# Query parts stored once, the value ring set in phase one, and phase one's weights loaded into sixteen tiles

## Chip, cores and metric

The kernel runs on one core of a Trainium2 chip. The time is the device time of one launch in microseconds, lower is better; a "time" here is the median of several launches, and a profiled launch gives the trace.

## The reference, cut to what matters

The input `x` has 32 sequences of 128 rows and 512 columns, `ctx_2048` the same shape. One decoder layer with three post-norm parts is computed, each followed by a layer norm of the sum with its input:

```python
x = _layernorm(x + _L0_attn_ref(x, Wq, Wk, Wv, Wo))        # 16 heads of 32, rope, causal softmax over 128 rows
x = _layernorm(x + _L0_xattn_ref(x, ctx, ctx, gamma))      # no projections
x = _layernorm(x + _L0_ffn_ref(x, w1, b1, ln_g, ln_b, w2, b2))

def _L0_xattn_ref(q, k, v, gamma):                         # q, k, v: (B, 128, 512)
    qh = q.reshape(B, 8, 16, 512); kh = ...; vh = ...      # 8 heads; 16 of the 128 rows are the head's width
    qk = jnp.einsum('bhdq,bhdl->bhql', qh, kh) / 4         # 512 x 512 scores for each head
    ret = jnp.einsum('bhql,bhdl->bhdq', softmax(qk), vh).reshape(B, 128, 512)
    return gamma * ret
```

The feed-forward part is a "1.58 bit" one: rows are normalized and quantized to 8 bit steps, weights to -1, 0 and 1; 512 to 2048 columns, silu, gelu, a layer norm over 2048, quantization again, and back to 512.

## The kernel before

The kernel has two phases, each a plan of its own. A `Plan` holds operations (`pl.op`) with an engine, a cost, the buffers they read and write and a priority. `Plan.run` sorts them while the program is built: it takes, again and again, the operation that can start first by the plan's own costs, ties within `slack` going to the lower priority, and issues it. Priorities are the batch's number plus an offset for each kind of operation (`OFF1`, `OFF2`), written out by hand. So the order of instructions on each engine is fixed when the program is built, and a change of an offset moves the order everywhere. Nearly all DMAs are issued by SP, in order: an SP instruction that waits holds up all that stand behind it. In the built program a DMA also waits for the DMA that stands eight places before it.

*Phase one* does self-attention for the 32 batches. `split_weight` (L302) loads the weights of Q, K, V and the output projection as sixteen 128x512 pieces; each is split into a high part (`hi`, a rounded copy by ACT L317 or DVE L315) and a low part (`lo`, the remainder, DVE L318). The staging tiles `wst` are four. `load` (L332) brings x twice, transposed (`xt`) and plain (`xs`). `stage_q` and `rope` project: twelve matmuls of 128x512 for each of q, k and v (`project`, L346). `stage_s` turns q and k (L430), makes scores (L447), masks and takes maxima on DVE (L459), exponentials on ACT (L465), and turns the weights again (L477). `stage_o` applies them to v (L496), projects with `wo` (L346 again, twelve matmuls), adds x and normalizes (x1, L519). `quantize_weights` makes the feed-forward weights beside this.

Cross-attention needs x1 and the context to more than bf16 precision, so `split3` (L349 to L365) writes each as three bf16 parts `sp` whose sum is the value: a cast on ACT (L354), a subtraction on POOL (L357), a cast (L359) and a subtraction (L361). A product of two such sums keeps six of its nine terms; they are stacked along the contraction, six times 16 rows:

```python
Q_PARTS = (0, 1, 2, 0, 1, 0)
K_PARTS = (0, 0, 0, 1, 1, 2)
for s, k in enumerate(parts):
    dma(kind, lambda s=s, k=k: nc.sync.dma_start(dst[s].rearrange("t h c -> h t c"), sp.t[:, k, :]), 131, (sp,), (), prio)
```

So a query or key goes to DRAM (`q_d`, `k_d`) as six 128 KB stores, each part as often as it is needed (L364).

*Phase two* does cross-attention and the feed-forward part. A batch has two groups `(b, g)` of four heads. Tiles `kp` and `qp` (four of each) have 96 rows of these parts and two more; they come by one DMA each (`load`, L656). `b1_` makes scores only for the row maxima: 16 units of one matmul (L677, 96 rows) and one DVE reduction (L681). `shift` turns the maxima (L691), splits them in two bf16 parts (`mhi`, `mlo`, L694, L695) and sends them by two 4 KB DMAs into the last two rows of `qp` (L700); the last two rows of `kp` hold ones. `b2_` then makes the scores a second time with the maximum subtracted by these two rows (L756, 98 rows), the exponential on ACT into tiles `ex` (L759) and the product with the values (L766). The value tiles `cT` are a ring of three, `vring`; half of a tile holds ones, so that the same matmul gives the denominator. Those ones are set by three POOL memsets (L616) once the pools of phase two are open. `final` divides and normalizes, `up_`, `gelu_` and `down_` do the feed-forward part (L925, L940 to L997, L1009).

*The seam.* When the last projection is issued, `early` (L577) frees the memory of the q, k and v weights, opens there the tiles `kp` and `qp`, and loads all four of each. All other memory of phase two lies over that of phase one, so a tile there can be written only when phase one's tiles and the stores from them are done.

Of the kernel before, what the change touches and what calls it, by code (L numbers as in the profile page):

```python
# [42 lines left out]
Q_PARTS = (0, 1, 2, 0, 1, 0)  # L43
K_PARTS = (0, 0, 0, 1, 1, 2)
# [19 lines left out]

CFG = dict(y0e='Pool', x2be='Pool', q2T=1, q1=2, tb2=3, boost=1.0, bank_mT='mx', bank_q1T='m', bank_z='m', bank_q2T='mx', bank_py='m', early=5, ssv=1, NQ=4, cT=3, f=2, num=1, x1=2, rden=2, x2=2, nb=32, mx=3, sT=3, acc=1, m=1, ex=8, mTe='DVE', acce='ACT', q1e='ACT', q2e='ACT', lne='Pool', ye='Pool', sce='Pool', mxw=1, stw=1, pair=1, z=3, xb=3, slack=0.05, last_lne='DVE', last_ye='DVE', last_sce='DVE', last_y0e='DVE', last_bank_mT='sT', last_bank_q1T='m', last_bank_z='sT', last_bank_q2T='mx', last_bank_py='sT', zm='PPPP', last_zm='FFFP', q1m='p', q2m='ad', last_q1m='d', last_q2m='ad')
OFF2 = {'SP.const': -264.67, 'x.kq': 390.3, 'SP.v': 77.29, 'PE.mx': -381.13, 'DVE.mx': 126.92, 'PE.mT': -632.22, 'DVE.mT': 8.23, 'SP.m': -156.28, 'PE.sT': -531.43, 'ACT.ex': -687.83, 'PE.pv': 37.38, 'ACT.acc': -737.17, 'SP.f': 49.63, 'SP.fd': 1119.71, 'SP.fn': 725.19, 'SP.fx': 343.0, 'DVE.rd': -172.57, 'SP.fr': -316.31, 'SP.fb': 17.98, 'Pool.y': -355.28, 'DVE.y': -82.99, 'Pool.yn': -277.59, 'DVE.c1': -57.25, 'Pool.c1': -358.01, 'Pool.c1m': -627.03, 'Pool.q1a': -78.8, 'Pool.x2b': 72.59, 'SP.q1T': -375.73, 'PE.c1': 39.79, 'DVE.z': -137.9, 'ACT.gelu': -406.78, 'DVE.nmu': -80.22, 'ACT.sq': -333.32, 'Pool.zn': -48.07, 'Pool.zt': 303.63, 'Pool.zb': -221.61, 'ACT.sq2': 252.58, 'DVE.am2': 91.79, 'Pool.c2': -682.87, 'Pool.c2m': -291.19, 'ACT.q2a': -262.61, 'DVE.q2a': -514.12, 'SP.q2T': 382.04, 'PE.c2': 86.97, 'DVE.c3': 17.23, 'Pool.c3': -278.83, 'Pool.c3n': 302.38, 'SP.out': 77.71, 'SP.kq': -42.69, 'DVE.yn': -735.62, 'DVE.c1m': 785.24, 'DVE.q1a': 467.22, 'DVE.zn': 550.15, 'DVE.zb': -508.13, 'DVE.c2m': -306.12, 'DVE.c3n': 99.96}
OFF1 = {'SP.x': 76.47, 'SP.w': -83.56, 'ACT.w': 1251.46, 'DVE.wl': 97.39, 'DVE.w': 1455.82, 'SP.wq': 258.11, 'ACT.wq': -501.07, 'DVE.wq': -718.11, 'PE.wq': 497.75, 'ACT.xh': -83.03, 'Pool.xl': -493.52, 'PE.qkv': 642.06, 'DVE.rope': -749.29, 'Pool.rope': 726.68, 'ACT.v': -277.88, 'SP.cx': 161.38, 'ACT.cs': 561.27, 'Pool.cs': 151.36, 'Pool.cs3': 444.12, 'SP.cs': -169.59, 'SP.ct': -341.75, 'ACT.ct': 5.76, 'SP.cv': 657.35, 'PE.qkT': -233.53, 'DVE.qkT': -713.26, 'PE.sc': 223.31, 'DVE.mask': -673.03, 'ACT.exp': 343.93, 'DVE.rd': 481.16, 'DVE.pr': 893.48, 'PE.prT': -342.18, 'DVE.prT': 602.51, 'ACT.prT': 121.56, 'Pool.pr': 38.32, 'PE.pv': 403.29, 'ACT.oh': 297.53, 'DVE.ol': -241.16, 'PE.wo': 645.28, 'DVE.y': -873.41, 'Pool.y': 255.11, 'Pool.x1': -113.85, 'SP.x1': 730.76, 'ACT.xs': 299.8, 'Pool.xs': -1039.81, 'Pool.xs3': 582.54, 'SP.xs': 975.4}
C1 = dict(pace=15.0, xs=4, pr=5, prT=7, ra=3, qkT=4, sp=3, spr=2, xhe='ACT', lne='Pool', s1e='Pool', s2e='ACT', cxl=-0.5, wq=3.0, nb=32, wst=4, mm=3, tr=3, sc=4, scc=1.1, po=1, pc=4, spe='ACT', cte='ACT', s3e='Pool', qke='DVE', pre=['DVE', 'DVE', 'Pool', 'Pool'], prTe=['DVE', 'ACT', 'ACT', 'ACT'], wl=24.0, slack=0.02)
# [14 lines left out]
class Plan:  # L83
# [34 lines left out]
    def op(self, kind, cost, fn, ins=(), outs=(), prio=0.0, lat=None, rel=0.0, join=False):  # L118
# [5 lines left out]
        o.deps, o.new = [], []  # L124
# [96 lines left out]
def decoder_kernel(ctx: ExitStack, tc: tile.TileContext, x, xT, cx, cxT, wqkT, wvT, woT, gamma,  # L221
# [28 lines left out]
    q_d = [dram.tile([6, XD, XH, D], BF16, tag=f"qd{b}", name=f"qd{b}") for b in range(NB)]  # L250
    c_d = [dram.tile([P, XD, NC * XH], F32, tag=f"cd{b}", name=f"cd{b}") for b in range(NB)]
    k_d = [dram.tile([6, XD, XH, D], BF16, tag=f"kd{b}", name=f"kd{b}") for b in range(NB)]


    with ExitStack() as st1:
# [38 lines left out]
        for name in ("mm", "tr", "sc", "po"):  # L294
            pl.tag(name, C1[name], group="bank")
        pl.tag("part", 2, wts, (P, 16))

        def dma(kind, fn, kb, ins=(), outs=(), prio=0.0, rel=0.0):
            pl.op("SP." + kind, max(0.55, kb / 340), fn, ins, outs, prio, 2.2 + kb / 340, rel)


        def split_weight(name, wts, src, cols):  # L302
# [3 lines left out]
            for j in range(cols // 512):  # L306
                sl = slice(j * 512, (j + 1) * 512)
                w = pl.buf("w")
                halves.append(w)

                def part(c, sl=sl, w=w):
                    t = pl.buf("wst")
                    dma("w", lambda: nc.sync.dma_start(t.t, src[:, c, sl]), 262, (), (t,), -1.0)
                    if c % 2:
                        pl.op("DVE.w", 0.34, lambda: nc.vector.tensor_copy(hi[:, c, sl], t.t), (t,), (w,), -1.0)  # L315
                    else:
                        pl.op("ACT.w", 0.48, lambda: nc.scalar.copy(hi[:, c, sl], t.t), (t,), (w,), -1.0)  # L317
                    pl.op("DVE.wl", 0.6, lambda: nc.vector.tensor_tensor(  # L318
                        lo[:, c, sl], t.t, hi[:, c, sl].bitcast(F32), ALU.subtract), (t,), (w,), -1.0)
                for c in range(NC):  # L320
                    part(c)
            return hi, lo, halves

        def en(e):
            return nc.vector if e == "DVE" else nc.gpsimd
# [6 lines left out]
        def load(b):  # L332
            at = b
            XS[b] = xt, xs = pl.buf("xt"), pl.buf("xs")
            dma("x", lambda: nc.sync.dma_start(xt.t, xT[b]), 262, (), (xt,), at, (b - 1.5) * C1["pace"])
            dma("x", lambda: nc.sync.dma_start(xs.t, x[b]), 262, (), (xs,), at, (b - 0.5) * C1["pace"])

        def project(kind, pq, parts, w, sl, wb, prio):
# [3 lines left out]
            for i in range(0, 12, m):  # L342
# [5 lines left out]
                pl.op("PE." + kind, 0.236 * m, mm, used + [wb], (pq,), prio)  # L348

        def split3(kind, v, dst, parts, prio):  # L350
# [12 lines left out]
            for s, k in enumerate(parts):  # L363
                dma(kind, lambda s=s, k=k: nc.sync.dma_start(dst[s].rearrange("t h c -> h t c"), sp.t[:, k, :]), 131,  # L364
                    (sp,), (), prio)  # L365

        def context(b):
# [3 lines left out]
            split3("cs", t, k_d[b], K_PARTS, at)  # L371
# [114 lines left out]
        def stage_o(b):  # L486
# [35 lines left out]
            split3("xs", x1, q_d[b], Q_PARTS, at)  # L522
# [46 lines left out]
        for b in range(NB1):  # L569
# [3 lines left out]
            stage_o(b)  # L573
        pl.slack = C1['slack']
        NQ = CFG['NQ']
        kring, qring = [], []

        def early():

            st2.close()  # L580
            qk = pool(ctx, "qk", side="right")
            for i in range(NQ):
# [5 lines left out]
                for t, d in ((k, k_d), (q, q_d))[:2 if i < min(CFG['early'], NQ) else 0]:  # L588
                    nc.sync.dma_start(t[0:NPR], d[i // 2][:, :, 4 * (i % 2):4 * (i % 2) + 4, :].rearrange(
                        "s t h c -> (s t) h c"))  # L590
# [494 lines left out]
```

## Time and profile before

| | |
|---|---|
| median of 3 launches | 1676.19 us (1674.02 to 1684.5) |
| profiled launch | 1675.28 us, its span 1673.5 us |
| busy: PE, DVE, ACT, POOL | 93%, 83%, 86%, 75% of the span |
| granted TensorE clock, mean | 0.973 |
| DMA | 258.71 MB, mean 155 GB/s; `kd<-sp` and `qd<-sp` 192 stores of 128 KB each |
| last projection of phase one, first score of phase two | 562.6 us, 585.55 us |

In the profile, times are microseconds from the span's start. PE is the matmul side of TensorE and PEld its weight loads; DVE is VectorE, ACT ScalarE, POOL GpSimd, and SPq stands for the DMA issues of SP. A line of the timeline is: start, duration, engine, line of the kernel and operation, output and input names, shapes, count, and in brackets how long the engine was idle before and what ended that. Matmul ends are modelled, so a busy PE may still run below its pace. The chain of waits is followed back from the last instruction. A DMA piece in it is the time from issue, or from the release, to landing.

### The profile page before, as it was taken

The page shows a single profiled execution, that of the slowest core. Times are in us where ns is not written, and L with a number is a line of the kernel's source. Part 1 is how long each engine was busy: PE and PEld are TensorE (multiplying, and loading weights), DVE is VectorE, ACT ScalarE, POOL GpSimd, SP SyncE. Part 2 cuts the span into 40 slices and gives each one's busy share as a digit, 9 for nine tenths or more (in the row PEclk, how much of TensorE's full clock was granted, in tenths as well). Part 3 has the DMA queues.
Part 4 walks back from the last instruction along what each step waited for, and adds up shares of the span by engine and source line. Part 5 has one row for each costly group of instructions (what it writes and reads, how often), then busy time and mean ns, then how long its engine had stood idle before and what let it go on. Part 6 is the DMA issues. An engine that isn't in the chain of part 4 may idle for free.

```text
span 1673.5 us, 30270 instructions
## 1 busy us (share of the span) xinstructions
PE 1551.4 (93%) x9540; PEld 785.0 (47%) x9540; DVE 1383.9 (83%) x3315; ACT 1432.7 (86%) x2950; POOL 1251.5 (75%) x1679
## 2 busy tenths in 40 slices
PE   6999999999999799999999999999999999999844
PEld 4878777777778333333333333333333333333211
DVE  6877776777777678899999989899899999998674
ACT  4889989899976367999989989899999999998963
POOL 3777778777787404679879888878978888986772
PEclk8999999999999799999999999999999999999977
DMA  6476677766664654355455345545544544544221
GB/s 226 163 236 232 226 231 244 255 233 214 209 208 153 185 177 122 93 129 145 113 133 147 105 129 139 131 115 139 142 110 128 153 110 134 149 122 123 69 62 50
DMA packets 235680, 258.71 MB, mean 155 GB/s; under 512 B 110072, under 2 KB 159224, under 8 KB 235136
## 3 DMA queue, kind: packets, MB, share of 16 engines
q1 hardware_dynamic: 235520, 256.78, 52.8%
q8 instruction: 75, 1.23, 0.3%
q14 instruction: 85, 0.70, 0.1%
HBM read 142.41 MB, written 92.81 MB: 141 GB/s over the span
## 4 chain that ended last, share of the span: by engine, by line
PE 41%; DVE 18%; POOL 16%; DMA 9%; ACT 8%; issue 7%; SPq 1%; POOLq 0%; ACTq 0%; DVEq 0%
PE banka L346 12%; DVE mt L681 8%; PE acc L766 7%; PE sT L756 6%; POOL z L972 6%; PE mx L677 5%; PE m L925 2%; DVE am L998 2%; PE banka L477 2%; DMA qd<-sp 2%; POOL z L794 2%; PE banka L447 2%; ACT pr L465 1%; ACT ex L759 1%; PE banka L496 1%
## 5 line engine op out<-in xcount | busy, mean ns | idle before, releaser
L681 DVE TENSOR_REDUCE mt<-mx 128x1 f32<-128x512 f32 x1024 | 643.4, 679 | 54.9 <-PE mx L677 52.9
L759 ACT ACTIVATE ex<-sT 128x512 f32<-128x512 f32 x1024 | 533.9, 615 | 77.9 <-PE sT L756 74.4
L677 PE MATMUL mx<-kp,qp 96*128 96x512 bf16 x1024 | 336.9, 386 | 21.5 <-DVE mt L681 17.7
L756 PE MATMUL sT<-qp,kp 98*128 98x512 bf16 x1024 | 320.7, 385 | 15.9 <-DMA qp<-mlo 13.3
L766 PE MATMUL acc<-ex,cT 128*32 128x512 f32 x2048 | 289.4, 637 | 0.0
L465 ACT ACTIVATE pr<-pr,nm 128x128 f32<-128x128 f32 x512 | 198.9, 394 | 4.1 <-DVE nm L459 4.1
L756 PEld LDWEIGHTS <-kp 98*128 98x128 bf16 x1024 | 90.3, 98 | 223.7 <-issue 125.1
L677 PEld LDWEIGHTS <-qp 96*128 96x128 bf16 x1024 | 96.3, 98 | 195.5 <-issue 95.1
L972 POOL TENSOR_TENSOR z<-z,bb_b 128x512 f32<-128x512 f32 x119 | 154.4, 1301 | 0.3
L972 POOL TENSOR_TENSOR z<-z,g_b 128x512 f32<-128x512 f32 x119 | 153.5, 1297 | 0.5
L459 DVE CUSTOM_DVE_ANT_0 pr<-banka,cmask 128x128 f32<-128x128 f32 x512 | 111.0, 286 | 35.9 <-PE banka L447 35.2
L1009 PE MATMUL m<-w2q,q2T 128*128 128x512 fp8e4 x464 | 116.7, 385 | 16.4 <-DMA q2T<-q 16.4
L766 PEld LDWEIGHTS acc<-ex,cT 128*32 128x32 f32 x2048 | 70.6, 184 | 114.1 <-issue 108.8
L925 PE MATMUL m<-w1q,q1T 128*128 128x512 fp8e4 x464 | 119.1, 378 | 2.7 <-DVE z L928 1.3
L1009 PEld LDWEIGHTS <-q2T 128*128 128x128 f16 x512 | 51.0, 101 | 104.5 <-DMA q2T<-q 34.9
L465 ACT ACTIVATION_READ_ACCUMULATOR pr<-pr,nm 128x1 f32 x512 | 98.0, 191 | 0.0
L794 POOL TENSOR_SCALAR z<-z,nmu,rs 128x512 f32<-128x512 f32 x119 | 94.5, 801 | 1.8
L361 POOL TENSOR_TENSOR sp<-spr,sp 128x512 bf16<-128x512 f32 x64 | 76.7, 1200 | 20.3 <-ACT sp L359 18.2
L928 DVE SCALAR_TENSOR_TENSOR z<-m,dq,b_b 128x512 f32<-128x512 f32 x116 | 85.0, 733 | 1.8 <-PE m L925 1.5
L925 PEld LDWEIGHTS <-q1T 128*128 128x128 f16 x512 | 49.2, 97 | 76.1 <-issue 19.9
L846 POOL TENSOR_TENSOR num<-num,rden 128x512 f32<-128x512 f32 x29 | 37.1, 1278 | 62.3 <-DMA rden<-rd 62.2
L346 PE MATMUL banka<-wqkh,xh 128*128 128x512 f32 x256 | 73.9, 411 | 10.3 <-ACT xh L388 10.3
(152 smaller groups left out, 3247.9 us busy)
## 6 DMA issues: line engine op xcount, KB each, us to landing
kd<-sp SPq DMA_DIRECT2D x192, 128.0 KB
qd<-sp SPq DMA_DIRECT2D x192, 128.0 KB
kp<-kd SPq DMA_DIRECT2D x64, 384.0 KB
qp<-qd SPq DMA_DIRECT2D x64, 384.0 KB
F<-f SPq DMA_DIRECT2D x64, 256.0 KB
xt<-in_xT SPq DMA_DIRECT2D x32, 256.0 KB
xs<-in_x SPq DMA_DIRECT2D x32, 256.0 KB
ct<-in_cxT SPq DMA_DIRECT2D x32, 256.0 KB
```

The lines of the kernel that those rows point to most:

```text
L346: nc.tensor.matmul(pq.t, parts[a].t[:, c, :], w[t][:, c, sl], start=k == 0, stop=k == 11)
L459: nc.vector.tensor_tensor_reduce(pr.t[:, c, :], sc.t[:, c * P:(c + 1) * P], cmask, -1.0, 3e38, ALU.add, ALU.min, nm.t[:, c:c + 1])
L465: nc.scalar.activation(pr.t[:, c, :], pr.t[:, c, :], AF.Exp, scale=-1.0, bias=nm.t[:, c:c + 1], accum_out=den.t[:, c:c + 1])
L677: nc.tensor.matmul(sc.t[:, j, :], q.t[0:NPR, h, (qc + j) * P:(qc + j + 1) * P], k.t[0:NPR, h, :], start=True, stop=True)
L681: pl.op("DVE.mx", 0.064 + 0.534 * W, lambda: nc.vector.tensor_reduce(mt.t[:, i:i + W], sc.t, AX.X, ALU.max), (sc,), (mt,), p, join=True)
L756: nc.tensor.matmul(sc.t[:, i, :], k.t[:, h, lc * P:(lc + 1) * P], q.t[:, h, :], start=True, stop=True)
L759: pl.op("ACT.ex", 0.052 + 0.426 * SW, lambda: nc.scalar.activation(ex.t[:, j:j + SW, :], sc.t, AF.Exp, scale=1.0 / XD ** 0.5), (sc,), (ex, ...
L766: nc.tensor.matmul(acc.t[32 * h:32 * h + 32, :], v.t[:, :, XH * lc + 4 * g + h], exs[h // 2].t[:, h % 2, :], start=lc == 0, stop=lc == NC - 1)
L794: pl.op(e + "." + p, cost + 0.1, lambda: en(e).tensor_scalar(o.t[:, sl], v.t[:, sl], sh.t, sc.t, ALU.add, ALU.mult), ins, outs, prio)
L925: nc.tensor.matmul(flat(pz)[:, i * 512:(i + 1) * 512], q1T.t[:, c, :], w1q[:, c, (n + i) * 512:(n + i + 1) * 512], start=c == 0, stop=c == ...
L972: pl.op(e + kind, 0.148 + 0.0021 * w if e == "Pool" else 0.05 + 0.00105 * w, lambda: en(e).tensor_tensor(t(), t(), other[:, sl], op), src, ...
L1009: nc.tensor.matmul(flat(py)[:, 0:D], q2T.t[:, c, :], w2q[:, c, :], start=c == 0, stop=c == NI - 1)
```

## The change

1. *Queries.* `q_d` holds the three parts once: three stores a batch in place of six. The tile `qp` is filled by three DMAs (48, 32 and 16 rows) that repeat a part three times, twice and once. Keys are still stored six times, as three operations of three, two and one DMAs, in another order of the terms.
2. *Weights of phase one.* The sixteen pieces go into sixteen tiles, seven of `prT`, five of `pr` and four of `wst` (the first two are not in use yet), so that no load waits for a split. The first `xt` gets a priority ahead of them. The low parts are split over DVE (ten) and POOL (six).
3. *Value ring.* The `cT` tiles move to the memory that `early` frees, and their ones are set there, in phase one.
4. *Carry.* Loads of the first four `kp` and `qp` become operations of phase one's plan that follow the stores they need and the last projection. `b1_` of the first group (`CARRY = 1`), with its `shift`, is planned in phase one, its scores in phase one's PSUM banks.
5. All offsets, and the `slack` of phase one (0.02 to 0.05), have new values.

```diff
-Q_PARTS = (0, 1, 2, 0, 1, 0)
-K_PARTS = (0, 0, 0, 1, 1, 2)
+Q_TIMES = (3, 2, 1)
+K_ROWS = (slice(1, 6, 2), slice(0, 5, 4), slice(2, 3))
...
-    q_d = [dram.tile([6, XD, XH, D], BF16, tag=f"qd{b}", name=f"qd{b}") for b in range(NB)]
+    q_d = [dram.tile([3, XD, XH, D], BF16, tag=f"qd{b}", name=f"qd{b}") for b in range(NB)]
...
+    def load_k(t, b, g):
+        nc.sync.dma_start(t[0:NPR], k_d[b][:, :, 4 * g:4 * g + 4, :].rearrange("s t h c -> (s t) h c"))
+
+    def load_q(t, b, g):
+        r = 0
+        for k, n in enumerate(Q_TIMES):
+            nc.sync.dma_start(t[r * XD:(r + n) * XD],
+                              q_d[b][k, :, 4 * g:4 * g + 4, :].unsqueeze(0).to_broadcast([n, XD, 4, D]))
+            r += n
...
+        stage = ["prT"] * C1["prT"] + ["pr"] * C1["pr"] + ["wst"] * C1["wst"]
...
                 def part(c, sl=sl, w=w):
-                    t = pl.buf("wst")
-                    dma("w", lambda: nc.sync.dma_start(t.t, src[:, c, sl]), 262, (), (t,), -1.0)
+                    tag = stage.pop(0)
+                    t = pl.buf(tag)
...
+                    dma("w", lambda: nc.sync.dma_start(flat_(), src[:, c, sl]), 262, (), (t,), -1.0)
...
-                    pl.op("DVE.wl", 0.6, lambda: nc.vector.tensor_tensor(
-                        lo[:, c, sl], t.t, hi[:, c, sl].bitcast(F32), ALU.subtract), (t,), (w,), -1.0)
+                    e = "Pool" if c == 3 or c == 1 and name != "wqk" else "DVE"
+                    pl.op(e + ".wl", 0.6 if e == "DVE" else 1.23, lambda: en(e).tensor_tensor(
+                        lo[:, c, sl], flat_(), hi[:, c, sl].bitcast(F32), ALU.subtract), (t,), (w,), -1.0)
...
-            dma("x", lambda: nc.sync.dma_start(xt.t, xT[b]), 262, (), (xt,), at, (b - 1.5) * C1["pace"])
+            dma("x", lambda: nc.sync.dma_start(xt.t, xT[b]), 262, (), (xt,), at if b else -1000.0, (b - 1.5) * C1["pace"])
...
-            for s, k in enumerate(parts):
-                dma(kind, lambda s=s, k=k: nc.sync.dma_start(dst[s].rearrange("t h c -> h t c"), sp.t[:, k, :]), 131,
-                    (sp,), (), prio)
+            for k, rows in enumerate(parts):
+                def put(k=k, rows=rows):
+                    for d in range(*rows.indices(6)):
+                        nc.sync.dma_start(dst[d].rearrange("t h c -> h t c"), sp.t[:, k, :])
+                n = len(range(*rows.indices(6)))
+                pl.op("SP." + kind, 0.55 * n, put, (sp,), (), prio, 2.2 + 0.4 * n)
...
-            split3("xs", x1, q_d[b], Q_PARTS, at)
+            split3("xs", x1, q_d[b], [slice(k, k + 1) for k in range(3)], at)
...
+        for i in range(NQ):
+            b, g = divmod(i, 2)
+            K[b, g], Q[b, g] = pl.buf("kp"), pl.buf("qp")
+            for t, load_, kind in ((K[b, g], load_k, "cs"), (Q[b, g], load_q, "xs")):
+                pl.op("SP.kq", 1.2, lambda t=t, load_=load_, b=b, g=g: load_(t.t, b, g), (), (t,), NB1 + b + 0.5 * g, 3.4,
+                      after=pl.kinds["SP." + kind][3 * b:3 * b + 3] + pl.kinds["PE.qkv"][-1:])
+            if i < CARRY:
+                b1_(b, g, NB1 + b + 0.5 * g)
...
         def early():
             st2.close()
             qk = pool(ctx, "qk", side="right")
+            for i in range(CFG["cT"]):
+                t = qk.tile([P, 2 * XD, NC * XH], F32, tag=f"cT{i}", name=f"cT{i}")
+                nc.gpsimd.memset(t[:, XD:], 1.0)
+                vring.append(t)
             for i in range(NQ):
...
                 nc.sync.dma_start(k[NPR:NROW], ones_d)
-                for t, d in ((k, k_d), (q, q_d))[:2 if i < min(CFG['early'], NQ) else 0]:
-                    nc.sync.dma_start(t[0:NPR], d[i // 2][:, :, 4 * (i % 2):4 * (i % 2) + 4, :].rearrange(
-                        "s t h c -> (s t) h c"))
...
-    vring = [cb.tile([P, 2 * XD, NC * XH], F32, tag=f"cT{i}", name=f"cT{i}") for i in range(CFG["cT"])]
-    for t in vring:
-        nc.gpsimd.memset(t[:, XD:], 1.0)
...
         for g in range(2):
-            b1_(b, g)
+            if 2 * b + g >= CARRY:
+                b1_(b, g, b + 0.5 * g)
```

## The prediction

> **What bounds the kernel now.** I read the page first: no engine is idle for long, so a gain must come from a place where the busy engines stand still together.
>
> ```profile
> span 1673.5 us, 30270 instructions
> PE 1551.4 (93%) x9540; PEld 785.0 (47%) x9540; DVE 1383.9 (83%) x3315; ACT 1432.7 (86%) x2950; POOL 1251.5 (75%) x1679
> ```
>
> Then the busy time by stage (columns: PE, PEld, DVE, ACT, POOL busy us, granted TensorE clock, DMA share, GB/s).
>
> ```profile
> 0.00:50.00 50.00, 33.46 (x209) 25.75 (x209) 32.09 (x88) 22.72 (x57) 20.57 (x32) 0.90 0.59 190
> 50.00:100.00 50.00, 50.00 (x418) 40.72 (x415) 40.64 (x181) 45.75 (x162) 36.53 (x40) 1.00 0.60 199
> 100.00:200.00 100.00, 99.02 (x824) 79.82 (x823) 74.38 (x312) 93.88 (x296) 76.77 (x91) 1.00 0.72 241
> ...
> 550.00:580.00 30.00, 24.68 (x107) 10.67 (x105) 22.98 (x43) 10.32 (x30) 15.37 (x22) 0.76 0.76 228
> 580.00:640.00 60.00, 51.95 (x263) 16.73 (x264) 42.09 (x74) 35.34 (x69) 6.84 (x13) 0.92 0.54 164
> ```
>
> The reader is to see two holes: the first 50 us, with half the matmuls of the next 50, and the seam near 580. In between phase one (to 562) runs on PE and ACT at once, and phase two (from 586) on PE, DVE and ACT, all over 90%.
>
> At the head the timeline gives the first batch, and the windows its clock (columns: PE busy, clock, DMA share, GB/s).
>
> ```profile
> 9.62 0.62 ACT L388 CAST xh<-xt 128x512 fp32r<-128x512 f32 x1 [2.69 <-DMA xt<-in_xT]
> 30.34 1.91 PE L346 MATMUL banka<-wvl,xh 128*128 128x512 f32 x4
> 32.17 1.71 PE L447 MATMUL banka<-qkT,qkT 32*128 32x128 f32 x32
> ```
>
> ```profile
> 20.00:22.00 2.00, 2.00 (x6) 0.50 0.58 163
> 34.00:36.00 2.00, 2.00 (x9) 1.00 0.65 172
> ```
>
> By 32.17 PE has done only the 36 projection matmuls of batch 0, each about 0.47 us instead of the 0.234 of later rows (a group of 20 takes 4.66).
>
> At the seam, the timeline:
>
> ```profile
> 574.43 4.06 PE L677 MATMUL mx<-kp,qp 96*128 96x512 bf16 x7 [0.21 <-DVE mt L681]
> 582.45 1.45 POOL L616 MEMSET cT<- 128x512 f32 x3 [9.06 <-DMA qd<-sp]
> 582.37 0.33 SPq L663 DMA_DIRECT2D cT<-cd  x1
> 583.42 0.57 SPq L700 DMA_DIRECT2D qp<-mlo  x1
> 585.55 1.44 PE L756 MATMUL sT<-qp,kp 98*128 98x512 bf16 x3 [7.06 <-DMA qp<-mlo]
> 586.22 1.58 ACT L759 ACTIVATE ex<-sT 128x512 f32<-128x512 f32 x3 [14.06 <-PE sT L756]
> ```
>
> The last wo matmul ends at 562.6. The last query store is issued by 577.4 and lands at 582.4; the value load waits for it, the two shift rows wait behind that load on SP, and PE starts the scores of phase two at 585.55, 23 us after phase one's last matmul. Only 24 maximum units (L677, L681) fill the hole.
>
> **The sum is made against** the profiled execution, 1675.3 us (span 1673.5 and 1.8 around it); the median of the three runs, 1676.2, is 0.9 above it.
>
> **Head.** All sixteen weight pieces get a tile of their own, so their loads no longer wait for a subtraction to free one of four tiles; xt of batch 0 is issued ahead of them. In 5 to 10 us the trace moved 329 GB/s, 0.8 us for a 256 KB piece. The first piece landed at 4.5 us; the last of xt, eight wqk pieces, ct and four wv pieces is thirteen places later, near 15. Six of sixteen subtractions go to POOL: DVE loses 6 x 0.69 = 4.1 us, POOL gains 6 x 1.27 = 7.6, and has the room (20.6 busy of 50). Working down the built order with these rows, batch 0's projections end near 22 us, or 26 if the clock stays at half, against 32. But xt of batch 1 now stands behind wo, cx and xs, the 20th load: 4.5 + 19 x 0.8 = 20 us (27 at the first slice's 226 GB/s). The built order puts 72 projection matmuls ahead of the first scores, not 36: scores near 31 to 35 us with 36 x 0.234 = 8.4 us more done. The lead is 9.4 us at most (1 us earlier as well); after the scores ACT must follow, and it was busy 5.3 us of the 10 between 40 and 50, so it can win some 4.7 + 1. I take -6; bounds -9.4 and +2 (xt late).
>
> The trace shows the clock at 0.50 in 20 to 22 and again at 28 to 32, after PE pauses of 3 and 2.6 us. The Trainium skill (TensorE: Matmul & The Clock Gate, The HAM clock gate) says that the clock opens after about 3.4 us of sustained work and closes after an idle window of that length. By that rule an unbroken feed would run the second half of batch 0 at full rate, and the head would gain nearer 9 than 6.
>
> **Middle of phase one.** PE's work for a batch is 48 x 0.234 + 1.10 + 1.01 + 6 x 0.435 = 15.95 us; from 100 to 500 it did 24 batches, 16.67 each: 23 us lost over 32 batches. Query stores drop from six to three a batch: 96 x 128 KB = 12.6 MB of 258.7 are gone, and at 0.6 an issue 1.9 us of SP time a batch. The other edits of the queue (key stores issued as three operations, still six DMAs) cost nothing, since SP is no bound. Query stores make 5.1% of the chain between 90 and 562, 24 us; half of it is the most to win. PE itself never waits for a DMA there (its listed waits, 11.6 us, are on ACT, DVE and POOL), and ACT at 94% keeps its pace. The carried group adds 16 x 0.22 = 3.5 us of PE. All offsets are new and I can't cost that order. Taken: -4; bounds -12 and +6.
>
> **Seam.** Three things move. The three memsets (1.45 us of POOL) go to the end of the last projection, ahead of POOL's work on batch 28, and stop waiting for stores. The first of 64 maximum groups (16 matmuls, 16 reductions of 0.6, a transpose, two splits, two 4 KB DMAs) runs among the last softmaxes. Its K and Q loads and the other three groups' (16 DMAs where eight were) stand on SP behind the last projection. This adds a wait: the carried group's first matmul waits for them, behind it on PE the transposes, pv and wo of batch 31. The loads are issued some 4 us after the last projection and land in 4 to 7.7 (the chain shows 7.67 for qp<-qd there); 24 wo matmuls and a transpose, 6 us, cover them, so 2 to 5 us may show, where before PE idled about 4 us for the same softmax.
>
> What does not go: the first ex tile lies over phase one's tiles, and the built program still has it wait for the last query store. From the last wo: ya, one reduction, statistics 2.9 us; POOL scale and x 1.8; two casts, a subtraction and another 3.6; three stores of 0.4 to 0.6 and 2.5 to 4.8 to land: 12.5 us, against 23.6 before (562.6 to 586.2). So -11; but 24 units were done by then and now 16, and to the first down projection the built order has 179 units from there, not 164: 15 x 0.217 = 3.3 us of PE back. Net -8; bounds -12 (POOL never backlogged) and 0 (POOL still busy with batches 28 to 30 when x is due, as x1 stores held it until 568.86 before).
>
> **Phase two.** Sixty later Q loads become three DMAs: 120 more issues of 0.43 us, 52 us of SP over 1,000 us. Queued behind each are the shift rows mhi and mlo, for which PE waits. They are covered as long as the ring of four K/Q tiles is a group ahead; at 92% busy engines and one batch per 32.1 us (666 to 1532 for batches 1 to 28) I take 0, bounds -5 and +15. Also -1 for tail and rest, bounds 4 either way.
>
> The row for an issue of qp<-qd is 0.43 us. The skill (DMA: Bandwidth & Descriptors, Bandwidth) speaks against the split: batch transfers to 1 MiB, since a DMA carries about 2 us fixed. By that rule 120 extra DMAs are 240 us of latency if they ran one after another; issued back to back they overlap, and by it the sum would change little.
>
> Sum: -6 - 4 - 8 - 1 = -19: 1675.3 - 19 = **1656 us**.
>
> **Rivals.** *Only the seam counts* (1664 to 1676, middle 1668): PE and ACT are both at their pace in phase one (15.5 us of ACT a batch), so head start and lighter DMA dissolve, leaving -8. For: ACT at 94%; PE waits on no DMA. Against: ACT's 4.7 us of idle time in 40 to 50.
> *All of it works* (1630 to 1646): -9 head, -12 middle, -11 seam, -2: 1641. For: 23 us are lost in phase one without a full engine. Against: retuned offsets would have to find them.
> *Slower*: the shift rows are issued late in phase two. Place: SP, behind three-part Q loads; price: two issues, 0.87 us, of PE waiting for qp<-mlo in each of 60 groups, 52 us, less 19: 1708. It decides from 0.6 us a group (19 + 17 over 60). For: PE and its weight loads already wait 31 us in all for mhi and mlo. Against: SP sits waiting for DVE mlo at L700 for 148.7 us, so it is mostly there in time.
> *The loads aren't at once*: in the built program a DMA waits for the one eight places before it. Eight pieces are in flight, twice the four of before; the gain of the head holds, so this has no time of its own.
>
> **How the numbers follow.** Forecast 0.48 (1646 to 1664), only the seam 0.24, all of it 0.15, slower 0.13. The median can tell about 1% from no change, 1659.4 and 1693: faster takes 0.15 and most of the forecast, 0.45; same has the rest of it, 0.03, and the seam's 0.24; slower 0.13 is the last rival. Range 1638 to 1680: it cuts the best of the second case and nearly all of the slower one.
>
> **What would show it.** First scores at 31 to 35 us after 72 projections; last wo near 553; ex some 12 us after it, with POOL's memsets before; batch pace of phase two still 32.1. Wrong if first ex comes 20 us after the last wo, if phase one needs 16.7 a batch and the head's lead is gone by 100 us, or if PE's waits for mlo exceed 60 us.

## The result, and the profile after

The changed kernel takes 1786.11 us (median of 4 launches, 1781.3 to 1787.59) against 1675.11 in the same comparison for the kernel before: the ratio of the means is 1.0652, with a 95% interval of 1.0599 to 1.0705. The forecast was 1656, its range ended at 1680. The profiled launch took 1781.3 us.

The same two lines of the page:

```profile
span 1779.5 us, 30353 instructions
PE 1581.2 (89%) x9540; PEld 788.5 (44%) x9540; DVE 1388.2 (78%) x3309; ACT 1433.0 (81%) x2950; POOL 1258.0 (71%) x1685
```

The busy times of DVE, ACT and POOL are those of before within 7 us; the span is 106 us longer. So the engines do the same work and stand still for longer. The busy time by stage says where (columns as in the prediction: PE, PEld, DVE, ACT, POOL, granted clock, DMA share, GB/s):

```profile
0.00:50.00 50.00, 39.49 (x224) 30.06 (x224) 36.09 (x101) 27.51 (x76) 35.32 (x45) 1.00 0.68 227
50.00:100.00 50.00, 49.05 (x468) 39.34 (x467) 40.28 (x175) 46.95 (x167) 33.85 (x38) 1.00 0.58 187
...
550.00:580.00 30.00, 12.40 (x73) 7.70 (x73) 13.35 (x24) 5.75 (x10) 11.53 (x15) 0.71 0.38 127
580.00:640.00 60.00, 51.35 (x227) 14.81 (x227) 41.37 (x71) 29.99 (x58) 0.00 (x0) 0.86 0.45 126
640.00:1550.00 910.00, 822.37 (x4150) 289.74 (x4147) 762.63 (x1291) 763.03 (x1151) 681.59 (x969) 0.95 0.52 116
```

The long stretch of phase two, 640 to 1550, was this before:

```profile
640.00:1550.00 910.00, 881.90 (x4600) 314.14 (x4599) 842.02 (x1428) 845.56 (x1280) 748.92 (x1066) 0.99 0.49 127
```

The head is better (39.49 us of PE where 33.46 were). The seam, meant to shrink, is emptier (12.40 where 24.68 were). And in the long stretch of phase two DVE and ACT each lose some 80 us of work against before. Its last two columns are the strange ones: before, the DMA engines were 0.49 busy and moved 127 GB/s; now they are 0.52 busy and move 116. More time in the engines for fewer bytes.

The chain of waits by engine, before:

```profile
PE 41%; DVE 18%; POOL 16%; DMA 9%; ACT 8%; issue 7%; SPq 1%; POOLq 0%; ACTq 0%; DVEq 0%
```

And after, by engine and by line:

```profile
PE 43%; DMA 18%; POOL 11%; ACT 10%; DVE 10%; issue 4%; SPq 3%; POOLq 0%; ACTq 0%; DVEq 0%
PE banka L436 11%; PE acc L798 8%; PE sT L788 7%; PE mx L301 6%; DMA rden<-rd 5%; POOL z L1004 4%; DVE mt L305 3%; DMA cT<-cd 3%; ACT pr L558 3%; PE m L1041 3%; DMA qp<-qd 2%; PE m L957 2%; PE banka L570 2%; SPq L286 2%; ACT ex L791 2%
```

DMA was 9% of the chain, 0.09 x 1673.5 = 151 us, and is 18%, 320 us. Transfers that were on nobody's path are on it now: rden (the reciprocal coming back), cT (values), qp. Pieces of that chain in order of time (start, duration, what):

```profile
750.62 8.15 DMA qp<-qd
...
786.70 9.01 DMA qp<-qd
...
862.70 13.47 DMA q2T<-q
...
907.99 7.59 DMA cT<-cd
```

Before, this was the longest piece of a transfer in phase two's chain:

```profile
1201.82 4.89 DMA rden<-rd
```

To split the loss by stage I read four marks from the timelines of the profiled launches: the end of the last q, k or v projection (the 562.6 given with the time before is the end of the output projection), the start of the first and of the last q1T transpose that SP issues, and the span's end.

| | last projection | to first q1T | first to last q1T | tail | span |
|---|---|---|---|---|---|
| before | 549.1 | 95.1 | 978.1 | 51.1 | 1673.5 |
| after | 540.7 | 121.1 | 1066.6 | 51.0 | 1779.5 |
| difference | -8.4 | +26.0 | +88.5 | -0.1 | +106 |

The tail is nothing, the head and the middle came out as forecast, and the seam and all of phase two went wrong together. What they share is the new Q load (L286).

### The profile page after: what moved, and what is told of

Read it like the earlier page. It is cut to its first block, busy times and chain, and to the rows that moved or that the text cites. A ratio compares the mean times of both kernels' runs of the same rounds, so it can differ in the third digit from the quotient of the medians.

```text
span 1779.5 us, 30353 instructions
## 1 busy us (share of the span) xinstructions
PE 1581.2 (89%) x9540; PEld 788.5 (44%) x9540; DVE 1388.2 (78%) x3309; ACT 1433.0 (81%) x2950; POOL 1258.0 (71%) x1685
## 4 chain that ended last, share of the span: by engine, by line
PE 43%; DMA 18%; POOL 11%; ACT 10%; DVE 10%; issue 4%; SPq 3%; POOLq 0%; ACTq 0%; DVEq 0%
PE banka L436 11%; PE acc L798 8%; PE sT L788 7%; PE mx L301 6%; DMA rden<-rd 5%; POOL z L1004 4%; DVE mt L305 3%; DMA cT<-cd 3%; ACT pr L558 3%; PE m L1041 3%; DMA qp<-qd 2%; PE m L957 2%; PE banka L570 2%; SPq L286 2%; ACT ex L791 2%
## 5 line engine op out<-in xcount | busy, mean ns | idle before, releaser
L305 DVE TENSOR_REDUCE mt<-mx 128x1 f32<-128x512 f32 x1008 | 636.4, 679 | 107.2 <-PE mx L301 104.1
L788 PE MATMUL sT<-qp,kp 98*128 98x512 bf16 x1024 | 323.6, 387 | 20.2 <-DMA qp<-mlo 11.3
L798 PE MATMUL acc<-ex,cT 128*32 128x512 f32 x2048 | 297.7, 657 | 18.5 <-DMA cT<-cd 18.3
L1041 PE MATMUL m<-w2q,q2T 128*128 128x512 fp8e4 x464 | 127.6, 413 | 24.4 <-DVE top L900 18.4
L1030 DVE TENSOR_REDUCE am<-z 128x1 f32<-128x2048 f32 x32 | 72.9, 2277 | 31.0 <-POOL z L1004 30.8
L840 POOL TENSOR_SCALAR rsa<-mv 128x1 f32<-128x1 f32 x64 | 13.8, 215 | 112.8 <-DVE mv L834 100.3
```

The lines of the kernel that those rows point to most:

```text
L305: pl.op("DVE.mx", 0.064 + 0.534 * W, lambda: nc.vector.tensor_reduce(mt.t[:, i:i + W], flat(sc).rearrange("p (a b) -> p a b", a=W), AX.X, ...
L788: nc.tensor.matmul(sc.t[:, i, :], k.t[:, h, lc * P:(lc + 1) * P], q.t[:, h, :], start=True, stop=True)
L798: nc.tensor.matmul(acc.t[32 * h:32 * h + 32, :], v.t[:, :, XH * lc + 4 * g + h], exs[h // 2].t[:, h % 2, :], start=lc == 0, stop=lc == NC - 1)
L1041: nc.tensor.matmul(flat(py)[:, 0:D], q2T.t[:, c, :], w2q[:, c, :], start=c == 0, stop=c == NI - 1)
```

## Experiments

**The theory.** A Q load reads `q_d[b][k, ...].unsqueeze(0).to_broadcast([n, XD, 4, D])`: the n copies, 3 or 2, are the slowest dimension, and the 16 rows stand inside. If the load is divided among the DMA engines along that dimension, only 3 or 2 of 16 engines carry it. It lands late, and whatever else passes those engines lands late behind it ("spread"). The rivals were the number of loads ("count": three where one was, with their issue time and the wait for the DMA eight places before) and the new offsets, carried group and seam ("order").

### The copies moved inside

```diff
-  q_d[b][k, :, 4 * g:4 * g + 4, :].unsqueeze(0).to_broadcast([n, XD, 4, D])
+  q_d[b][k, :, 4 * g:4 * g + 4, :].unsqueeze(1).to_broadcast([XD, n, 4, D])
```

The rows of K are stored in the matching order. Three loads stay, with the same bytes.

> The changed kernel with its three Q loads a group kept, same bytes and same order of work on all five engines, but inside each load the copies of a row lie next to each other (16 rows outermost, the 3 or 2 copies inside) instead of the 3 or 2 copies outermost; the K rows are stored to match. Theory 'spread' (a load whose slowest dimension is 3 or 2 is carried by 3 or 2 of the 16 DMA engines, lands late and holds up the transfers behind it): the loss of phase two goes, 1650 to 1675 us, PE's chain waits for rden<-rd, cT<-cd and qp<-qd fall to the 4 to 5 us they had before the change. Rival 'count' (three DMAs where one was, their issue time and the wait for the eighth DMA before): nothing changes, 1780 to 1792. Rival 'order' (offsets, carried group, seam): nothing changes, 1780 to 1792.

Measured: 1661.53 us, ratio to before 0.9942 (0.9919 to 0.9965). One changed pattern takes away 125 us (1786.11 to 1661.53); "count" and "order" fall as main causes. Against the kernel before, the whole change is now worth 0.6%. The same two views for this kernel, the stretch of phase two and the chain by engine:

```profile
640.00:1550.00 910.00, 885.39 (x4631) 318.14 (x4630) 842.05 (x1431) 851.04 (x1284) 753.30 (x1073) 0.99 0.50 127
```

```profile
PE 45%; POOL 16%; DVE 15%; ACT 12%; DMA 7%; issue 4%; SPq 1%; POOLq 0%; ACTq 0%; DVEq 0%
```

DVE, ACT and the bytes moved are back at the rate of before, and DMA is 7% of the chain.

### Six loads of 16 rows

```diff
-  nc.sync.dma_start(t[r * XD:(r + n) * XD],
-                    q_d[b][k, :, 4 * g:4 * g + 4, :].unsqueeze(0).to_broadcast([n, XD, 4, D]))
+  for i in range(n):
+      nc.sync.dma_start(t[(r + i) * XD:(r + i + 1) * XD], q_d[b][k, :, 4 * g:4 * g + 4, :])
```

> The changed kernel with six Q loads a group of 16 rows and 64 KB each in place of three (stored once as before, same order of work). 'Spread': each load has 16 rows outermost and the loss goes although there are 192 DMAs more, 1655 to 1695 us. 'Count': worse than the changed kernel, since the three added DMAs a group cost as much again, 1850 to 1900. 'Order': 1780 to 1800.

Measured: 1669.87 us (ratio 0.9985, 0.9967 to 1.0004). Twice as many loads, and 116 us faster than the changed kernel, with K stored as there. "Count" does have a price: 192 loads more cost 8.3 us against the version before this one, 0.04 us each.

### Storing undone, and storing alone

The first puts six stored copies and one 96-row load back into the changed kernel; the second puts the once-stored Q with its three loads, copies outermost, into the kernel before and changes nothing else there but the order of K's parts, to match. The first edit, cut to what matters:

```diff
- q_d = [dram.tile([3, XD, XH, D], ...
+ q_d = [dram.tile([6, XD, XH, D], ...
...
- for k, n in enumerate(Q_TIMES):
-     nc.sync.dma_start(t[r * XD:(r + n) * XD],
-                       q_d[b][k, :, 4 * g:4 * g + 4, :].unsqueeze(0).to_broadcast([n, XD, 4, D]))
...
+ nc.sync.dma_start(t[0:NPR], q_d[b][:, :, 4 * g:4 * g + 4, :].rearrange("s t h c -> (s t) h c"))
...
- split3("xs", x1, q_d[b], [slice(k, k + 1) for k in range(3)], at)
+ split3("xs", x1, q_d[b], [slice(0, 3), slice(3, 5), slice(5, 6)], at)
```

> The changed kernel with the storing of Q undone: six copies are written, one 96-row load a group; order of the other engines' work unchanged. 'Spread' and 'count' both: 1655 to 1680 us, the gain that the prediction gave to head and seam less its share for the lighter stores. 'Order': 1775 to 1795.

> The kernel before with only the storing of Q changed: stored once, three loads a group with the 3 or 2 copies outermost, everything else and the order of the other engines' work as before. 'Spread' and 'count': about as slow as the changed kernel, 1760 to 1800 us. 'Order': 1665 to 1680.

Measured: 1691.3 us and 1803.46 us. The second settles that this part alone makes a kernel slow: without any of the other edits it costs 131 us, and its phase two (first to last q1T) is 1104.6 us long. Which wait shows it depends on the order: here it is the shift rows, for which PE's second scores wait 79.6 us (who waited, for what, us in total, times, longest):

```profile
PE sT L768 <- DMA qp<-mlo: 79.6, 22, 15.1
```

The first missed its expectation by 11 us. Its phase two is sound (974.2), but its last projection ends at 562.9, 23 us later than with three stores (539.8 with the copies inside). In the changed order, three more stores a batch cost much more than the 4 us that the prediction gave them.

### Loads by themselves

A kernel that only loads. Each of 13 forms was issued alone, four times; the table has eleven of them.

> Only loads, nothing of the layer is computed: 13 forms of a load from device memory, each issued alone after the one before has landed, four times over; then four of them with a 256 KB load of 128 rows issued right behind. All 48-row forms carry the same 192 KB (48 rows of 4 KB). A small VectorE copy marks when a load is there, a GpSimd copy when the 256 KB behind it is. Theory 'spread': the head of the kernel before moved 329 GB/s, 20 GB/s for each of 16 engines, so the n-outermost form takes about 192 KB / n / 20 GB/s beyond a fixed part: against the plain 48 rows, n = 2 lands 4.2 us later, n = 3 2.6, n = 4 1.8, n = 6 1.0, n = 8 0.6, n = 16 none; copies inside (16 rows outermost) none; and the 256 KB behind n = 3 or n = 2 lands late by about the same. Rivals 'count' and 'order': all forms of 192 KB land within 0.4 us of each other and the load behind them does too.

The table gives the median time from the start of the issue to the start of the copy that waits for the load.

| form | KB | us | | form | KB | us |
|---|---|---|---|---|---|---|
| 48 plain rows | 192 | 2.88 | | 6 copies outermost | 192 | 4.25 |
| 3 copies inside | 192 | 3.31 | | 8, 12 copies outermost | 192 | 3.38, 3.41 |
| 2 copies outermost | 192 | 5.99 | | 16 copies outermost | 192 | 3.28 |
| 3 copies outermost | 192 | 5.85 | | 16 plain rows | 64 | 2.06 |
| 4 copies outermost | 192 | 3.97 | | 96 plain rows | 384 | 3.43 |

The 96 rows are twice the bytes in little more than half the time. How many engines work is in the DMA column of the windows, the mean busy share of 16 engines (last two columns: share, GB/s). The first window lies inside a load with 2 copies outermost, the second inside one with 3, the third inside one of 96 plain rows:

```profile
17.00:20.00 3.00, 0.00 (x0) 0.00 (x0) 1.00 0.12 44
23.50:26.50 3.00, 0.00 (x0) 0.00 (x0) 1.00 0.18 60
48.50:49.50 1.00, 0.00 (x0) 0.00 (x0) 1.00 0.68 229
```

Two engines of 16 are a share of 0.125 and three are 0.188; the windows show 0.12 and 0.18. The rate for one engine is the same in all three, 44 / (16 x 0.12) = 23, 60 / (16 x 0.18) = 21 and 229 / (16 x 0.68) = 21 GB/s, so nothing is wrong with the reading itself. The trace's semaphore events agree. Between issue and landing a DMA's semaphore is counted up 3 times with 2 copies outermost, 4 times with 3, 5 with 4, 7 with 6, 9 with 8, 13 with 12, and 16 times for every form with 16 or more rows or copies outermost: one signal for each engine at work, and one more where fewer than 16 are. (The Trainium skill, DMA: Bandwidth & Descriptors, "Why a DMA increments its semaphore by 16 and not by 1", says what the one more is: the issuer writes the share of the idle engines at once.)

The transfer behind suffers as well. The same events give the landing of a 256 KB load of 128 rows that SP issues right behind the Q form, four times each, from its own issue to its first and to its last engine:

| Q form ahead of it | first engine, us | last engine, us |
|---|---|---|
| 48 plain rows | 2.72 to 2.76 | 2.95 to 3.06 |
| 3 copies inside | 2.91 to 3.03 | 3.20 to 3.32 |
| 2 copies outermost | 2.19 to 2.41 | 5.84 to 6.08 |
| 3 copies outermost | 2.46 to 2.62 | 5.48 to 5.74 |

The first of its engines is done as early as ever, the last one 2 to 3 us late. How many are late shows that they are the engines that it shares with the load ahead: behind 2 copies outermost, 14 of the 16 signals come within 2.9 us and exactly two at 5.7 to 6.1 us, in all four repetitions; behind 3 copies, 13 come within 3.3 us and exactly three at 4.5 to 5.7 us.

The sizes were only partly as expected: 2 copies and 3 copies cost the same, and 16 copies outermost and copies inside 0.4 us more than plain rows.

### The kernel before with storing once and copies inside

> The kernel before with only the storing of Q changed, as in the run that did this alone, but the copies inside each load (16 rows outermost). Order of the other engines' work as before. 'Spread': the earlier end of phase one that the n-outermost version had (last wo matmul 12 us earlier than before) stays and phase two keeps 32.1 us a batch: 1655 to 1668 us. 'Count': phase two still loses for its 120 more loads, 1690 to 1800.

Measured: 1662.34 us (ratio 0.9934, 0.9901 to 0.9967). The lighter stores bring the last projection forward from 549.1 to 535.8, 13.3 us, in an order that was not touched; phase two, at 983.8, gives 5.7 of it back.

### Half of the cause

Only the three-copy load gets its 16 rows outermost; the two-copy load stays as changed.

> The changed kernel with only the first of the three Q loads (3 copies, 192 KB) given its 16 rows outermost; the second (2 copies, 128 KB) stays with the copies outermost. 'Spread': in the run of loads alone both forms kept 2 and 3 of the 16 DMA engines busy; with the first one spread, the two engines that the second still uses carry 64 KB of it a tile where they carried 128 KB of both, so part of the loss stays: 1675 to 1735 us, between 1661.5 and 1786. If the loss came with the three-copy load alone, 1660 to 1668; if it came with the two-copy load alone, 1780 to 1790.

Measured: 1710.29 us. First to last q1T is 972.6, 1010.1 and 1066.6 us with none, one and both loads in the bad form: 37.5 us for the first and 56.5 more for the second. The first is the load of 2 copies and 128 KB, the second that of 3 copies and 192 KB: the loss goes with the bytes put on the few engines, 2 to 3, as far as two steps can show it.

### Loads that nothing waits for

Two spare loads behind each of the 60 Q loads of phase two, into a tile that nothing reads, on top of the version with copies inside; once with the copies outermost (shown), once inside (`unsqueeze(1)`).

```diff
+ for k, n in ((0, 3), (1, 2)):
+     part = q_d[b][k, :, 4 * g:4 * g + 4, :]
+     nc.sync.dma_start(spare[k][0:n * XD], part.unsqueeze(0).to_broadcast([n, XD, 4, D]))
```

> The changed kernel with the copies inside each Q load, and in phase two, behind each of its 60 group loads of Q, two further loads into a spare tile that nothing reads: the same 192 KB and 128 KB with the copies outermost. Nothing waits for these. If the loss comes from what a load on two or three DMA engines does to the transfers behind it (rden, cT, K, the transposes), most of the loss comes back although Q itself is loaded well: 1725 to 1790 us. If it came from the late landing of Q itself, this is as the same two loads with the copies inside, within 10 us.

> The control: the same spare loads, bytes and places, with the 16 rows outermost, so that both are carried by 16 engines. It prices 120 more loads of 320 KB a group in all: 1663 to 1685 us by either theory.

Measured: 1860.17 us and 1691.35 us. Both are beyond their ranges, but the contrast is clear: 169 us lie between the same bytes in two patterns, and no engine reads the tile. So Q's own late landing isn't needed for the loss; what the narrow loads do to others suffices. PE's waits for the values show it (who waited, for what, us in total, times, longest); first outermost, then inside:

```profile
PE acc L810 <- DMA cT<-cd: 58.4, 11, 11.2
```

```profile
PE acc L810 <- DMA cT<-cd: 5.0, 3, 3.8
```

The landings in the full kernels say the same. These are medians over phase two (from 640 us on), us from an issue's start to the last engine's signal. For q2T the last three batches are left out, as their semaphores have 17 or 18 signals where all others have 16:

| transfer | before | after | copies inside | with spare, outermost | with spare, inside |
|---|---|---|---|---|---|
| cT, values | 3.55 | 7.63 | 4.00 | 7.47 | 4.55 |
| q2T, transpose | 5.18 | 8.43 | 4.95 | 8.82 | 5.47 |
| qp, shift rows | 1.72 | 2.60 | 1.73 | 3.25 | 2.40 |
| qp, Q (before: 384 KB in one) | 5.05 | 8.19 | 4.63 | 4.60 | 4.86 |

Only the last row was edited from before to after, and in the fourth column it is as good as ever while the three others are about as late as in the changed kernel or later.

Not every transfer is late: it goes with a narrow load in flight. In the changed kernel, from 640 us on, median landings are (number of transfers in brackets):

| transfer | no narrow Q load in flight at its issue | one in flight |
|---|---|---|
| cT, values | 2.94 (11) | 8.15 (19) |
| kp, K | 4.07 (47) | 8.63 (11) |
| rden | 3.69 (19) | 8.44 (12) |
| mlo, shift row | 1.73 (33) | 5.57 (27) |

So rden can stand on the path although its median over all batches is that of before (4.00 us, 4.01 before). With the copies inside, cT lands after 2.82 us with no Q load in flight and 4.38 with one, rden after 3.86 and 4.35.

One caution: SP is held too. In the outermost version of the spare loads it waits 48.5 us in all for a spare load to land before it reuses the tile (13.4 in the inside version), and in both kernels with narrow loads it spends longer on the q2T issues (last section). So a part of the 169, and of the changed kernel's loss, is SP held up and not the shared engines. No run separates the two. What "count" had in mind, SP waiting for an earlier Q load to land, is small: 15 us in the changed kernel's phase two.

### The other parts, in the good form

Each of the next runs starts from the version with the copies inside (1661.53), but for the last row of the table, which starts from the kernel before with storing once (1662.34).

> The changed kernel with the copies inside each Q load, and the first group of maxima not carried into phase one but left where phase two puts it. If the carried group and the early shift rows make the seam shorter, as the prediction had it (net 8 us with the memsets), 1664 to 1672 us against 1661.5; if the seam's gain comes from the early end of phase one and the memsets alone, 1658 to 1663.

> The changed kernel with the copies inside each Q load, and the head undone: the weight pieces go through four tiles again and all sixteen subtractions run on VectorE (the planned order of phase one shifts with it). If the head's lead of 8 us at the end of phase one is real and lasts, 1667 to 1672 us; if PE and ScalarE dissolve it ('only the seam counts'), 1660 to 1663.

> The changed kernel with the copies inside each Q load, and the three memsets of the value ring set back to the start of phase two, as before the change; everything else as it is. If the memsets' early place shortens the seam, 1664 to 1670 us, and the first scores of phase two again start behind the value load; if the shift rows of the carried group have taken them off the path, 1660 to 1663.

> The kernel before with two parts of the change: Q stored once with the copies inside each load, and the head (sixteen tiles, xt of batch 0 first, six subtractions on GpSimd); offsets, seam and carried group as before. If the two gains add (storing once alone gave 1662.3, the head at most 8 more): 1654 to 1660 us. If the order of before cannot use the head's lead: 1660 to 1666.

> The changed kernel with the copies inside each Q load, and K stored once as well (three stores a batch where six were), its rows for a group brought in by three loads with the 16 rows outermost. Order of the other engines' work unchanged. If an added load costs little when it is spread, phase two keeps its pace and phase one, where PE is busy 393 of 400 us, wins 0 to 4 us: 1656 to 1663 us. If added loads cost something by their number ('count'), the two more a group show: 1668 to 1690.

The marks are those of the profiled launches, which took 1673.96 with K stored once and 1669.82 with the head in the kernel before, 5.5 and 4.2 us above the medians shown.

| run | us | last projection | to first q1T | first to last q1T |
|---|---|---|---|---|
| changed, copies inside | 1661.53 | 539.8 | 95.0 | 972.6 |
| carried group off | 1692.58 | 540.0 | 90.1 | 1007.7 |
| head off | 1676.93 | 549.2 | 100.0 | 976.0 |
| ring memsets late | 1661.29 | 540.4 | 93.5 | 973.5 |
| K stored once too | 1668.44 | 534.8 | 97.6 | 987.5 |
| before, storing once, copies inside | 1662.34 | 535.8 | 91.6 | 983.8 |
| the same with the head | 1665.58 | 539.7 | 96.5 | 980.6 |

The kernel before with nothing but storing once, copies inside, is as fast as the whole change in that form (1662.34 and 1661.53): the other parts together show no gain. The memsets' place is worth nothing. The head is worth 9.4 us at the last projection and 15 at the end under the changed offsets, more than expected; under those of before the last projection comes 3.9 us later with it and the time is 3 us longer. The run without the carried group is outside both of its expectations and doesn't price it: the first q1T comes earlier, and the 35 us are lost later in phase two, whose order the planner drew up anew from offsets written for the carried group. That cause was not followed up. Storing K once gives phase one 5 us and takes 15 in phase two of the profiled launch, and its median is 7 us longer; 120 spread loads more are not free.

## Why the prediction was wrong, step by step

**The term that failed is "Phase two", taken as 0 with bounds of -5 and +15; it measured +88.5.** The step costed the split load by its issues, 120 x 0.43 us of SP that would be covered, and asked whether SP was in time. It never asked how many DMA engines carry the load. What the runs showed in its place: a load with 2 or 3 copies outermost keeps 2 or 3 of 16 engines busy and lands 8.2 us after its issue, other transfers issued meanwhile land late with it, and with the copies inside the same step measures -5.5 (972.6 where 978.1 were). The trace of before held no large load with so short an outer dimension (its four small loads of ones, 2 rows outermost, signal 3 times), and the upper bound should not have come from issue times alone.

The rule was to be had. The Trainium skill (DMA: Bandwidth & Descriptors, Rules for kernel authors, "Use all 16 engines") says that the slowest dimension of the patterns decides how many engines take part and that a leading broadcast of c copies holds a DMA to c engines at most. The shares of 0.12 and 0.18 agree for 2 and 3 copies. The prediction cited the Bandwidth section of the same page instead, for the size of a batch; there the runs agree with the forecast's reading, since 192 more loads cost 8.3 us and not 2 us each.

**The seam.** Forecast net -8; from the last projection to the first q1T it measured +26.0, and -0.1 with the copies inside. Two steps failed. The loads for the carried group were to land in 4 to 7.7 us and cost 2 to 5 us of PE at most. Its three Q loads landed 7.4, 9.4 and 8.9 us after their issues (5.3, 4.9 and 4.5 with the copies inside), PE waited 6.0 us for them, and the shift rows then came late as well. Here it is mostly their issue: mlo is issued at 577.66 us, and at 563.50 with the copies inside, where the wait is 3.85 us. The two waits in the changed kernel:

```profile
553.51 0.58 PE L301 MATMUL banka<-kp,qp 96*128 96x512 bf16 x1 [6.02 <-DMA qp<-qd]
...
581.68 1.44 PE L788 MATMUL sT<-qp,kp 98*128 98x512 bf16 x3 [11.30 <-DMA qp<-mlo]
```

With the copies inside, the last wo matmul ends at 556.3 and the first ex comes at 569.4, 13.1 us later; forecast were 553 and 12 us. That part was right, in the good form (19.2 us in the bad one). But the first scores, at 566.3 and 19.2 us ahead of before, lead to a first q1T only 9.4 us ahead: half is given back within the first batch, where the prediction had charged 3.3 us. Of the 19.2, 9.3 come from the earlier last projection, so the seam gained 9.9 up to the first scores and lost all of it by the first q1T. Why it was lost there stays open.

**Head and middle.** Forecast -6 and -4; the last projection ended 8.4 us earlier. The first scores came at 33.77 us, in the range of 31 to 35, after 72 projections. The sum of -10 came out near by luck, for its terms weren't right: undoing the head costs 9.4 us there, the upper bound (the granted clock of the first 50 us is 1.00, with the head off 0.93, before 0.90), and the stores alone are worth 13.3 in the old order and 23 in the new. As both together gave 8.4, the new offsets by themselves must have cost phase one some of that; this is the remainder of a sum and not a run.

**The rivals.** "Slower" had the right sign and the wrong place. It put the price on the shift rows behind SP's issues, and PE's wait for mlo is 11.3 us in all, where it needed more than 60; before, the row was this (total, times, longest):

```profile
PE sT L756 <- DMA qp<-mlo: 13.3, 7, 7.1
```

In the kernel before with storing once alone, that very wait is 79.6 us, but the price is not one of issues: with the copies inside, and as many loads, it is 7.8. With the copies outermost mlo lands 5.57 us after its issue (median of 13) when a narrow load is in flight and 1.72 (46) when none is. "Only the seam counts" and "all of it works" were both without the mechanism. Had the load been spread, the forecast of 1656 would have been 5.5 us off, and the gain of 10.5 us (1672.04 to 1661.53) about half of the 19 that were forecast.

**The batch pace** of phase two, batches 1 to 28, is 35.3 us where 32.1 was forecast; with the copies inside it is 32.0.

## What to carry to other kernels

Before a load is split or broadcast, read its pattern from the slowest dimension: in the 13 forms tried here that count, up to 16, was the number of DMA engines that carried it, by their signals, and two engines moved 44 GB/s where a spread load moved 229. Put the 16 or more rows outermost and the copies inside, and lay out the other operand to match. When a trace, as here, shows a higher DMA share at fewer bytes a second and late landings of transfers that weren't touched, look for one narrow load ahead of them in the queue.

## What was not expected of the hardware

Three copies outermost were no faster than two (5.85 and 5.99 us for 192 KB), although three engines were busy and four copies took 3.97; six took more than four. The engines of the 3-copy load don't finish together (signals at 4.4 to 5.1, 5.4 to 6.1 and 5.7 to 6.2 us), those of the 2-copy load do, within 0.2 us. Why is not explained.

Other transfers of the kernel before were narrow already: den, num and rden signal 9 times, and so do all 384 stores of Q and K parts, so 8 engines carry each, the 8 heads being their slowest dimension. rden is the one that comes to stand longest on the path in the changed kernel (5% of the chain). No run widened them.

SP itself was held in phase two. The instruction that issues the q2T transpose (columns: count, shortest, median, longest ns) took nearly twice as long in the changed kernel as with the copies inside:

```profile
L1035 SPq DMA_TRANSPOSE q2T<-q x32: 1322/5768/11358, 746.0 to 1763.9; - x32
```

```profile
L1040 SPq DMA_TRANSPOSE q2T<-q x32: 1322/3042/4499, 715.9 to 1642.6; - x32
```

Before the change:

```profile
L1003 SPq DMA_TRANSPOSE q2T<-q x32: 1322/3017/6431, 718.4 to 1657.8; - x32
```

The medians differ by 2.7 us and the 32 issues together by 71 us (162.1 and 91.0), in which SP issues nothing else. It goes with the bad form in the other runs too: 6.08 us with it in the kernel before, 6.17 with the spare loads outermost, 3.98 with half of it. Within the changed kernel the median is 7.13 us when a Q load is in flight (20 issues) and 1.90 when none is (12); with the copies inside 3.42 (19) and 1.89 (13). Why a load in flight makes the transpose's issue longer was not tested.
